# Choosing each expert's eight tokens by a threshold, and collecting the experts' outputs through DRAM, in a convolution-attention-expert kernel

## The chip, the cores and the metric

The kernel runs on one core of a Trainium2 chip. The metric is the device time of one execution in microseconds (us). Three runs of the kernel before the change took 2435.75, 2436.49 and 2438.75 us; their median, 2436.49 us, is the time to which the changed kernel is compared. The core's engines are TensorE (PE, matrix products and transposes), VectorE (DVE), ScalarE (ACT), GpSimd (POOL) and SyncE (SP, which here only issues DMAs). ACT issues DMAs too.

## What is computed

The input is x of shape (4, 128, 64, 64): 4 images of 128 channels and 4096 positions. Layer 0 is a group norm and an attention over the 4096 positions of an image. Layer 1 works on the positions as tokens of 128 numbers: a running (cumulative) attention with 8 heads, and then an expert layer in which every expert chooses its tokens:

```python
logits = jnp.einsum('bsd,ed->bse', x, gate_w) + gate_b
probs = jax.nn.softmax(logits, axis=1)
vals, idx = jax.lax.top_k(probs.transpose(0, 2, 1), K)
...
pooled = jnp.einsum('bked,bke->bed', gathered, topv)
...
h = jax.nn.gelu(jnp.einsum('ebd,edh->ebh', h, weight1), approximate=False)
...
out = jnp.einsum('ebh,eho->ebo', h, weight2)
...
outputs = outputs.at[jnp.arange(Bn)[:, None], flat_idx].add(weighted)
```

There are 64 experts (E), each takes the K = 8 tokens of an image with its highest gate logits, the softmax runs over the 4096 tokens, and x stands here for the layer-normed tokens. An expert sums its eight tokens by their probabilities into one row (pooled), passes that row through two matrices (128 to 512, GELU, 512 to 128), and adds the result, times each token's probability, to its eight tokens.

## The kernel before

Everything is in float32. Layer 0 fills the first 1460 us or so; the change does not touch it. It leaves all tokens in SBUF in the tile `t`, and for every query the sum of its softmax row in `rows`. Layer 0 leaves out the row maximum of the softmax; `test_rows` (L645) tests that all these sums lie in a safe interval and writes the verdict to `inside`. At the very end every engine loads `inside` into a register (L1304), and if it is 0 everything is computed again by a slower general path (L1305 to L1308), which calls `layer1("g_", False)`. With the inputs used here `inside` is 1. The argument `ready` of `layer1` is True in the first, fast call.

`layer1` first runs a loop over 32 blocks of 512 tokens (`loop`, L1025; n counts blocks, NB = 32, 8 blocks an image). The order of PE's instructions in it is that of the program text (`tc.manual_schedule`); the order of all other instructions, here and later, comes from a list scheduler. `gate_logits` (L929) leaves the gate logits of images 2p and 2p+1 in `lgs[p]`, a tile of 128 partitions (64 experts of two images) by 4096 tokens, and the eight largest of every 512 in `cand[p]`.

The choice has these steps, for p = 0 inside the loop (n = 18 to 26) and for p = 1 after it:

- `select` (L942): the eight largest (`top`) of the 64 candidates, minus the largest (`ng`), and six more small DVE instructions which replace in `cand[p]` every candidate that is not among the eight by a number that no logit has.
- `pick_mark` (L964), for each block k: `match_replace` on DVE copies the logits into `left` and overwrites in it one occurrence of each value of `cand[p][:, k, :]`. So ties are resolved as top_k does.
- `pick_exp` (L973): ACT takes exp(logit - maximum) in place and adds up the softmax denominator.
- `pick_keep` (L980): DVE keeps the exponentials that are marked and sets the others to 0.
- `pick_turn` and `pick_sum`: PE transposes the kept weights, DVE multiplies them by the tokens' inverse deviations (`ct`), PE adds up the weighted tokens (`pp`).

Then the pools of the loop are closed, and the space takes 19 weight buffers of 512 KB, with `wks` and `wvs` 21 (NW). `load_expert` (L1110) loads an expert's two matrices on SP's queue into buffer e modulo 21; the first 21 loads are issued as space comes free, load e + 21 when expert e has been used.

The experts are taken in 16 groups g of four (QG = 4, EG = 16). `first(g)` (L1209) multiplies the pooled rows by the four first matrices and copies the result from PSUM (`hr`, ACT). `turn(g)` (L1222) transposes it (`htr`, PE), adds the bias (`hs`, DVE) and takes the GELU (ACT). `second(g)` (L1237) multiplies by the second matrices (`po`), copies to SBUF (`og`, DVE, two buffers), issues the four loads that the group's buffers are free for, and sends the group's 16 rows (4 experts, 4 images, 512 bytes each) to `eos[p]`, where partition z*64 + e holds expert e's output for image 2p + z: four DMAs of four rows, two on SP's queue and two on ACT's (L1254). The loop (L1261) also multiplies one block of `lgs` by the softmax denominator's inverse `rden` on ACT (L1272), and turns one or two blocks of `t` to channel-major form (`backs`, L1151: four PE transposes into `otr` and one copy, by ACT or DVE). `HB` = 16 of the 32 turned blocks come before the group loop: seven while the last logits are made, nine in the loop over k (L1177).

Every engine executes its own instructions in order, and so do the DMA queues' issuing engines: an issue on ACT or SP that waits holds up what stands behind it. The built program gives every DMA that SP and ACT issue one of eight completion semaphores in turn; a DMA is only issued when the one that used its semaphore before has landed.

At the end (L1275 to L1301) DVE adds the second bias to `eos`, PE multiplies the outputs by the probabilities block by block (`sct`), DVE adds this to `t`, and SP stores the result, 24 DMAs of 256 or 512 KB.

Of the kernel before, what the change touches and what calls it, by code (L numbers as in the profile page):

```python
# [8 lines left out]
F32 = mybir.dt.float32  # L9
AF = mybir.ActivationFunctionType  # L10
# [3 lines left out]
P = 128  # L14
# [4 lines left out]
def conv_attn_hybrid_kernel(  # L19
# [623 lines left out]
    inside = resid.tile([P, 1], mybir.dt.int32, tag="inside", name="inside")  # L643

    def test_rows(sb, ps):  # L645

        ends = sb.tile([P, 4], F32, tag="ends", name="ends", bufs=1)
        nc.vector.tensor_reduce(ends[:, 0:1], rows, AX.X, ALU.min)
        nc.vector.tensor_reduce(ends[:, 1:2], rows, AX.X, ALU.max)
        nc.vector.tensor_scalar(  # L650
            out=ends[:, 2:3], in0=ends[:, 0:1], scalar1=1e-20, scalar2=None, op0=ALU.is_ge
        )
        nc.vector.tensor_scalar(
            out=ends[:, 3:4], in0=ends[:, 1:2], scalar1=1e25, scalar2=ends[:, 2:3],
            op0=ALU.is_le, op1=ALU.mult,
        )
        good = ps.tile([P, BLK], F32, tag="kv", name="good")
        nc.tensor.matmul(good[:, 0:1], all_ones, ends[:, 3:4], start=True, stop=True)
        nc.vector.tensor_scalar(  # L659
            out=inside, in0=good[:, 0:1], scalar1=float(P), scalar2=None, op0=ALU.is_ge  # L660
        )
# [11 lines left out]
    def layer1(pre, ready):  # L673

        with ExitStack() as kept, ExitStack() as l1:
# [223 lines left out]
            den = lgp.tile([P, B // 2, NBLK], F32, tag="den", name=f"{pre}den")  # L899
            rden = lgp.tile([P, B // 2], F32, tag="rden", name=f"{pre}rden")  # L900

            total = lgp.tile([P, C], F32, tag="total", name=f"{pre}total")
            gmv, grs, xgs, xts, picks, cts, lefts = {}, {}, {}, {}, {}, {}, {}
# [38 lines left out]
            def select(p):  # L942

                flat = cand[p].rearrange("p k e -> p (k e)")
                top = gp.tile([P, 8], F32, tag="top", name=f"{pre}top_{p}")
                nc.vector.max(out=top, in_=flat)
                ng = gp.tile([P, 1], F32, tag="ng", name=f"{pre}ng_{p}")
                nc.vector.tensor_scalar_mul(ng, top[:, 0:1], -1.0)
                sel = gp.tile([P, NBLK * 8], F32, tag="sel", name=f"{pre}sel_{p}")
                nc.vector.match_replace(  # L950
                    out=sel, in_to_replace=top, in_values=flat, imm_value=-LOWEST
                )
                nc.vector.tensor_scalar(
                    out=sel, in0=sel, scalar1=1e38, scalar2=None, op0=ALU.is_ge
                )
                nc.vector.tensor_mul(flat, flat, sel)
                nc.vector.tensor_scalar(
                    out=sel, in0=sel, scalar1=1.0, scalar2=3e38, op0=ALU.subtract, op1=ALU.mult
                )
                i = nc.vector.tensor_add(flat, flat, sel)  # L960
                picks[p] = ng
                return i.ins

            def pick_mark(p, k, left):  # L964

                lefts[p, k] = left
                i = nc.vector.match_replace(
                    out=left, in_to_replace=cand[p][:, k, :], in_values=lgs[p][:, bass.ts(k, BLK)],
                    imm_value=LOWEST,
                )  # L970
                return i.ins

            def pick_exp(p, k):  # L973
                lg = lgs[p][:, bass.ts(k, BLK)]
                i = nc.scalar.activation(
                    lg, lg, AF.Exp, bias=picks[p], accum_out=den[:, p, k : k + 1]
# [3 lines left out]
            def pick_keep(p, k):  # L980
                lg = lgs[p][:, bass.ts(k, BLK)]
                nc.vector.scalar_tensor_tensor(
                    out=lg, in0=lefts.pop((p, k)), scalar=-3.3e38, in1=lg,
                    op0=ALU.is_le, op1=ALU.mult,
                )
# [39 lines left out]
            def loop():  # L1025
# [3 lines left out]
                for n in range(NB):  # L1029
# [18 lines left out]
                    with ExitStack() as order:  # L1048
# [3 lines left out]
                        if 0 <= k0 < NBLK:  # L1052
                            left = gp.tile([P, BLK], F32, tag="left", name=f"{pre}left_0_{k0}")
                            order.enter_context(tc.issue_after(pick_mark(0, k0, left)))
# [48 lines left out]
            fs = pool("l2fs", 2)  # L1103
            ps_a = pool("l2a", 4, space=PSUM)
# [19 lines left out]
            eos = [fo.tile([P, C], F32, tag=f"eo{p}", name=f"{pre}eo_{p}") for p in range(B // 2)]  # L1124
# [45 lines left out]
            backs(2, nc.scalar)  # L1170
# [6 lines left out]
            for k in range(NBLK + 1):  # L1177
# [9 lines left out]
                if turns and turns[0] < HB:  # L1187
                    backs(1, nc.scalar)
# [48 lines left out]
            def second(g, hs):  # L1237
# [12 lines left out]
                by = og.rearrange("(u w) o -> w u o", u=QG)  # L1250
                for p in range(B // 2):
                    for z in range(2):
                        at = z * E + g * QG
                        (nc.scalar if p else nc.sync).dma_start(  # L1254
                            out=eos[p][at : at + QG, :], in_=by[2 * p + z]
                        )
# [4 lines left out]
            for g in range(EG):  # L1261
# [9 lines left out]
                with tc.issue_after(gelu):  # L1271
                    nc.scalar.activation(probs, probs, AF.Copy, scale=rden[:, p : p + 1])  # L1272
                second(g, hs)
            backs(len(turns), nc.vector)
            for eo in eos:  # L1275
                nc.vector.tensor_add(eo, eo, fb2s)

            for p in range(B // 2):

                for k0, OB in ((0, 1), (1, 1), (2, 2), (4, 2), (6, 1), (7, 1)):  # L1280
                    for k in range(k0, k0 + OB):
# [4 lines left out]
                        for z in range(2):  # L1286
                            half = slice(z * E, (z + 1) * E)
                            nc.tensor.matmul(
                                pss[z], eos[p][half, :], lgs[p][half, bass.ts(k, BLK)],
# [6 lines left out]
                    for z in range(2):  # L1296
                        n = (2 * p + z) * NBLK + k0
                        nc.sync.dma_start(
# [65 lines left out]
```

## Time and profile before

| What | Value |
|---|---|
| Median of three runs | 2436.49 us |
| The profiled execution: time / span of its instructions | 2434.62 / 2432.9 us |
| PE busy | 2360.8 us, 97% of the span |
| DVE, ACT, POOL busy | 1504.9, 1213.7, 304.1 us |
| `match_replace` of 512 logits (L967) | 0.676 us, plus 0.086 us to load the eight values |
| exp of 512 logits (L975) | 0.722 us, plus 0.188 us to read the sum |
| scaling of 512 probabilities on ACT (L1272) | 0.710 us |
| DMAs to `eos` | 64 of 2 KB |
| weight loads | 64 of 512 KB |

Busy time is the time in which an engine executes; the span is from the first instruction to the last. PE's matmuls are pipelined and their ends are modelled, so that a busy PE can still have been waiting in part. Times of single instructions are given as us from the start of the span. A row of the timeline gives start, duration, engine, line, operation, output and inputs, shapes and count, and in brackets the idle time of the engine before it and what ended it. A row of the waits gives who waited for whom, the total, how many times, and the longest.

### The profile page before, as it was taken

To read this page: it belongs to the slowest core of one execution; us is meant where nothing else is said; L and a number is where in the kernel's file an instruction comes from. 1 tells how busy PE (TensorE), PEld (TensorE's weight loads), DVE (VectorE), ACT (ScalarE), POOL (GpSimd) and SP (SyncE) were. 2 spreads that over 40 slices of the span, in tenths; PEclk is the share of its full clock that TensorE was granted. 3 is DMA by queue.
4 is the path that set the end of the run, shared out by engine and by line. 5 is a ranking of instruction groups with operands and counts; after the bars stand their busy time and mean duration, and the time that the engine had idled before them with its cause. 6 is when DMAs were issued, how large, how long until landed. Compare 5 with 4: busy or idle time off the path is not lost. (4 is left out here: it accounts for less than half of the span.)

```text
span 2432.9 us, 45864 instructions
## 1 busy us (share of the span) xinstructions
PE 2360.8 (97%) x19482; PEld 1569.3 (65%) x19482; DVE 1504.9 (62%) x2619; ACT 1213.7 (50%) x1631; POOL 304.1 (13%) x338
## 2 busy tenths in 40 slices
PE   6999999999999999999999998999999999999886
PEld 3567767677778677677777774555555555555543
DVE  5666666666656666655555555666666677776623
ACT  4454444444443544444434335666666666656531
POOL 0000000000000000000000002433333333333100
PEclk9999999999999999999999999999999999999899
DMA  2200120000100000200000001121211211112576
GB/s 75 79 22 11 26 61 1 11 18 22 49 23 1 22 14 18 54 13 1 1 1 1 1 1 36 37 54 37 49 43 38 53 37 50 42 37 54 201 261 255
DMA packets 61704, 110.09 MB, mean 45 GB/s; under 512 B 10288, under 2 KB 35632, under 8 KB 61488
## 3 DMA queue, kind: packets, MB, share of 16 engines
q1 hardware_dynamic: 59520, 105.48, 15.0%
q8 instruction: 154, 2.52, 0.4%
q10 hardware_dynamic: 1968, 1.58, 0.2%
q14 instruction: 62, 0.51, 0.1%
HBM read 85.40 MB, written 8.91 MB: 39 GB/s over the span
## 5 line engine op out<-in xcount | busy, mean ns | idle before, releaser
L513 PE MATMUL av<-pr,am 64*128 64x512 f32 x4096 | 1051.2, 592 | 0.7 <-ACT pr L492 0.7
L495 DVE TENSOR_TENSOR acc<-acc,pr 128x1024 f32<-128x1024 f32 x480 | 586.9, 1223 | 443.5 <-ACT pr L492 443.2
L492 ACT ACTIVATE pr<-sc 128x1024 f32<-128x1024 f32 x512 | 523.5, 1023 | 671.0 <-PE sc L488 602.2
L513 PEld LDWEIGHTS av<-pr,am 64*128 64x128 f32 x4096 | 636.9, 187 | 253.0 <-issue 31.1
L488 PE MATMUL sc<-e,e 64*128 64x512 f32 x2048 | 608.0, 592 | 0.0
L488 PEld LDWEIGHTS sc<-e,e 64*128 64x128 f32 x2048 | 315.3, 187 | 103.4 <-issue 15.9
L725 PE MATMUL pk<-xt,wks 128*128 128x512 f32 x512 | 241.5, 611 | 6.5 <-DVE inside L659 4.2
L843 PE MATMUL pv<-wvs,xt 128*128 128x512 f32 x512 | 227.3, 597 | 2.1 <-ACT v L847 2.1
L847 ACT ACTIVATE v<-pv 128x512 f32<-128x512 f32 x256 | 152.7, 597 | 70.3 <-PE pv L843 70.2
L727 ACT ACTIVATE ks<-pk 128x512 f32<-128x512 f32 x256 | 148.5, 597 | 60.1 <-PE pk L725 59.8
L843 PEld LDWEIGHTS pv<-wvs,xt 128*128 128x128 f32 x512 | 96.6, 191 | 122.1 <-issue 112.6
L831 DVE TENSOR_TENSOR em<-em,rb 128x1024 f32<-128x1024 f32 x64 | 79.0, 1235 | 146.1 <-DMA rb<-rd 146.1
L725 PEld LDWEIGHTS pk<-xt,wks 128*128 128x128 f32 x512 | 91.3, 191 | 113.1 <-issue 80.9
L822 POOL TENSOR_TENSOR em<-et,mask 128x1024 f32<-128x1024 f32 x64 | 122.4, 1934 | 85.9 <-ACT et L809 85.9
L96 POOL TENSOR_SCALAR xg<-t,gmv,grs 128x128 f32<-128x128 f32 x120 | 95.1, 805 | 288.6 <-DVE grs L92 229.7
L879 PEld LDWEIGHTS po<-v,em 64*64 64x64 f32 x4096 | 111.6, 133 | 27.3 <-DVE before L869 26.7
L879 PE MATMUL po<-v,em 64*64 64x128 f32 x4096 | 119.6, 271 | 0.3 <-issue 0.3
L733 POOL MEMSET ew<- 128x1024 f32 x1 | 1.0, 952 | 942.1 <-PE pa L455 942.1
L781 DVE RECIPROCAL rr<-rr 128x512 f32<-128x512 f32 x32 | 107.3, 3353 | 1.1
L766 ACT ACT_TABLE_LOAD x24 | 30.8, 1283 | 119.0 <-DVE ss L765 119.0
L767 POOL COPY state<-mm 128x1 f32<-128x1 f32 x32 | 20.6, 644 | 502.3 <-DVE mm L761 502.3
L869 DVE TENSOR_TENSOR before<-before,pt 128x128 f32<-128x128 f32 x256 | 72.6, 284 | 9.6 <-PE pt L859 3.8
(185 smaller groups left out, 2101.9 us busy)
## 6 DMA issues: line engine op xcount, KB each, us to landing
rb<-rd SPq DMA_DIRECT2D x128, 256.0 KB
fw<-in_fw_dram SPq DMA_DIRECT2D x58, 512.0 KB
t<-in_xtok_dram SPq DMA_DIRECT2D x32, 256.0 KB
e<-ee SPq DMA_DIRECT2D x63, 128.0 KB
x<-in_x_dram SPq DMA_DIRECT2D x14, 512.0 KB
out_dram<-t SPq DMA_DIRECT2D x16, 256.0 KB
out_dram<-t SPq DMA_DIRECT2D x8, 512.0 KB
e<-ee SPq DMA_DIRECT2D x63, 64.0 KB
```

The lines of the kernel that those rows point to most:

```text
L96: i = engine.tensor_scalar(out=dst, in0=t[:, chunk, :], scalar1=mean, scalar2=rs, op0=ALU.subtract, op1=ALU.mult)
L488: nc.tensor.matmul(sc[:, u, :], e2[halves[u], p, :], e1[halves[u], :], start=True, stop=True)
L492: nc.scalar.activation(pr, sc, AF.Exp)
L495: added.append(nc.vector.tensor_add(acc, acc, pr).ins)
L513: nc.tensor.matmul(av, am[h, j, :], pr[h, u, :], start=(j == 0), stop=(j == NCH - 1))
L725: nc.tensor.matmul(pk, wks[:, h, :], xt, start=True, stop=True)
L727: nc.scalar.activation(ks, pk, AF.Silu)
L781: inverse = nc.vector.reciprocal(rr, rr).ins
L822: nc.gpsimd.tensor_tensor(em, eq.unsqueeze(2).to_broadcast([P, 2 * NH, H2]), mask.unsqueeze(1).to_broadcast([P, 2 * NH, H2]), ALU.mult,)
L843: nc.tensor.matmul(pv.rearrange("p h d -> p (h d)"), xt[:, bass.ts(2 * q + s, P)], wvs[:, bass.ts(m, BLK)], start=True, stop=True,)
L847: last = nc.scalar.activation(v[:, bass.ts(m, HPB), :], pv, AF.Silu).ins
L879: nc.tensor.matmul(po[s * H2 : (s + 1) * H2, u, q, :], aas[q][half, s, h, :], vs[2 * q + s][half, h, :], start=(q == 0 and h == 0), stop=F ...
```

## The change

Five things are changed, all in `layer1` and for the first call unless said otherwise.

1. **Choice.** `select` stops after `top` and `ng`; the eighth largest logit is kept as `eighth[p]`. `pick_mark` does nothing but name the tile `left`; `pick_exp` writes the exponentials into `left` and leaves the logits; `pick_keep` keeps an exponential where its logit is at least `eighth[p]`. With `ready` False all is as before.
2. **Count.** A logit equal to the eighth would be chosen too, so the chosen are counted: in the group loop ACT takes the sign of a block of kept exponentials into a PSUM tile and adds it up (`count`). At the end DVE and one matmul test that no expert has more than eight, and `inside` becomes the product of this test and of the old one (now `within`). So the load of `inside` on SP, which stood early in the program, now stands ahead of the stores.
3. **Scaling.** The multiplication by `rden` goes from ACT to DVE.
4. **Outputs.** A group's `og` is written whole to a DRAM tile `ogd` (64 KB, one DMA on ACT's queue), for all groups but the last. When group 14 is written, four DMAs on SP's queue read 60 rows each from there into `eos`; the last group's 16 rows go directly, two DMAs on SP and two on ACT. `eos` is one tile, and the bias is added by one DVE instruction.
5. **Turned blocks and stores.** Two of the seven `backs` ahead of the choice go into the loop over k, whose copies must follow the exp of that k; and every second store of the result is issued by ACT in place of SP.

```diff
@@ -641,6 +641,7 @@
     inside = resid.tile([P, 1], mybir.dt.int32, tag="inside", name="inside")
+    within = resid.tile([P, 1], F32, tag="within", name="within")
@@ -657,7 +658,7 @@
         nc.vector.tensor_scalar(
-            out=inside, in0=good[:, 0:1], scalar1=float(P), scalar2=None, op0=ALU.is_ge
+            out=within, in0=good[:, 0:1], scalar1=float(P), scalar2=None, op0=ALU.is_ge
         )
@@ -897,10 +903,12 @@
+            count = lgp.tile([P, B // 2, NBLK], F32, tag="count", name=f"{pre}count")
             rden = lgp.tile([P, B // 2], F32, tag="rden", name=f"{pre}rden")
             total = lgp.tile([P, C], F32, tag="total", name=f"{pre}total")
-            gmv, grs, xgs, xts, picks, cts, lefts = {}, {}, {}, {}, {}, {}, {}
+            gmv, grs, xgs, xts, picks, eighth, cts, lefts = {}, {}, {}, {}, {}, {}, {}, {}
@@ -942,10 +950,13 @@
                 flat = cand[p].rearrange("p k e -> p (k e)")
-                top = gp.tile([P, 8], F32, tag="top", name=f"{pre}top_{p}")
+                top = gp.tile([P, 8], F32, tag=f"top{p}", name=f"{pre}top_{p}")
                 nc.vector.max(out=top, in_=flat)
-                ng = gp.tile([P, 1], F32, tag="ng", name=f"{pre}ng_{p}")
-                nc.vector.tensor_scalar_mul(ng, top[:, 0:1], -1.0)
+                ng = gp.tile([P, 1], F32, tag=f"ng{p}", name=f"{pre}ng_{p}")
+                i = nc.vector.tensor_scalar_mul(ng, top[:, 0:1], -1.0)
+                picks[p], eighth[p] = ng, top[:, 7:8]
+                if ready:
+                    return i.ins
                 sel = gp.tile([P, NBLK * 8], F32, tag="sel", name=f"{pre}sel_{p}")
@@ -958,12 +969,13 @@
                 i = nc.vector.tensor_add(flat, flat, sel)
-                picks[p] = ng
                 return i.ins
...
                 lefts[p, k] = left
+                if ready:
+                    return None
                 i = nc.vector.match_replace(
@@ -973,16 +985,22 @@
                 i = nc.scalar.activation(
-                    lg, lg, AF.Exp, bias=picks[p], accum_out=den[:, p, k : k + 1]
+                    lefts[p, k] if ready else lg, lg, AF.Exp, bias=picks[p],
+                    accum_out=den[:, p, k : k + 1],
                 )
...
                 lg = lgs[p][:, bass.ts(k, BLK)]
-                nc.vector.scalar_tensor_tensor(
-                    out=lg, in0=lefts.pop((p, k)), scalar=-3.3e38, in1=lg,
-                    op0=ALU.is_le, op1=ALU.mult,
-                )
+                left = lefts.pop((p, k))
+                if ready:
+                    nc.vector.scalar_tensor_tensor(
+                        out=lg, in0=lg, scalar=eighth[p], in1=left, op0=ALU.is_ge, op1=ALU.mult
+                    )
+                else:
+                    nc.vector.scalar_tensor_tensor(
+                        out=lg, in0=left, scalar=-3.3e38, in1=lg, op0=ALU.is_le, op1=ALU.mult
+                    )
@@ -1051,7 +1069,9 @@
                             left = gp.tile([P, BLK], F32, tag="left", name=f"{pre}left_0_{k0}")
-                            order.enter_context(tc.issue_after(pick_mark(0, k0, left)))
+                            marked = pick_mark(0, k0, left)
+                            if marked is not None:
+                                order.enter_context(tc.issue_after(marked))
                         if 1 <= k0 <= NBLK:
@@ -1101,6 +1121,9 @@
             fs = pool("l2fs", 2)
+            dram2 = l1.enter_context(
+                tc.tile_pool(name=pre + "l2dram", bufs=1, space=bass.MemoryType.DRAM)
+            )
             ps_a = pool("l2a", 4, space=PSUM)
@@ -1121,7 +1144,8 @@
-            eos = [fo.tile([P, C], F32, tag=f"eo{p}", name=f"{pre}eo_{p}") for p in range(B // 2)]
+            eos = fo.tile([P, B // 2, C], F32, tag="eo", name=f"{pre}eo")
+            ogd = dram2.tile([(EG - 1) * P, C], F32, tag="og", name=f"{pre}ogd")
             fb2s = fo.tile([P, C], F32, tag="fb2s", name=f"{pre}fb2s")
@@ -1167,7 +1191,6 @@
             select(1)
-            backs(2, nc.scalar)
             pp = ps_p.tile([P, C], F32, tag="pp", name=f"{pre}pp_1")
@@ -1184,8 +1207,10 @@
                     pick_sum(1, k - 1, pp, k == 1, k == NBLK)
-                if turns and turns[0] < HB:
-                    backs(1, nc.scalar)
+                for _ in range(2 if k < 3 else 1):
+                    if turns[0] < HB:
+                        with tc.issue_after(exp):
+                            backs(1, nc.scalar)
             divisors(1)
@@ -1247,13 +1272,19 @@
                     load_expert(g * QG + u + NW)
-                by = og.rearrange("(u w) o -> w u o", u=QG)
-                for p in range(B // 2):
-                    for z in range(2):
-                        at = z * E + g * QG
-                        (nc.scalar if p else nc.sync).dma_start(
-                            out=eos[p][at : at + QG, :], in_=by[2 * p + z]
-                        )
+                if g + 1 < EG:
+                    nc.scalar.dma_start(out=ogd[bass.ts(g, P), :], in_=og)
+                    by, of, queues = ogd, slice(0, (EG - 1) * QG), (nc.sync, nc.sync)
+                else:
+                    by, of, queues = og, slice(g * QG, E), (nc.sync, nc.scalar)
+                if g + 2 >= EG:
+                    by = by[: (of.stop - of.start) * QW].rearrange("(e w) o -> w e o", w=QW)
+                    for p in range(B // 2):
+                        for z in range(2):
+                            queues[p].dma_start(
+                                out=eos[z * E + of.start : z * E + of.stop, p, :], in_=by[2 * p + z]
+                            )
@@ -1268,12 +1299,31 @@
                 probs = lgs[p][:, bass.ts(k, BLK)]
-                with tc.issue_after(gelu):
-                    nc.scalar.activation(probs, probs, AF.Copy, scale=rden[:, p : p + 1])
+                if ready:
+                    ones_of = ps_a.tile([P, BLK], F32, tag="kv", name=f"{pre}chosen_{g}")
+                    with tc.issue_after(gelu):
+                        nc.scalar.activation(
+                            ones_of, probs, AF.Sign, accum_out=count[:, p, k : k + 1]
+                        )
+                nc.vector.tensor_scalar_mul(probs, probs, rden[:, p : p + 1])
                 second(g, hs)
             backs(len(turns), nc.vector)
-            for eo in eos:
-                nc.vector.tensor_add(eo, eo, fb2s)
+            if ready:
+                chosen = fs.tile([P, 4], F32, tag="chosen", name=f"{pre}chosen", bufs=1)
+                nc.vector.tensor_reduce(chosen[:, 0:2], count, AX.X, ALU.add)
+                nc.vector.tensor_reduce(chosen[:, 2:3], chosen[:, 0:2], AX.X, ALU.max)
+                nc.vector.tensor_scalar(
+                    out=chosen[:, 3:4], in0=chosen[:, 2:3], scalar1=8.5, scalar2=None, op0=ALU.is_le
+                )
+                good = ps_a.tile([P, BLK], F32, tag="kv", name=f"{pre}good")
+                nc.tensor.matmul(good[:, 0:1], all_ones, chosen[:, 3:4], start=True, stop=True)
+                nc.vector.tensor_scalar(
+                    out=inside, in0=good[:, 0:1], scalar1=float(P), scalar2=within,
+                    op0=ALU.is_ge, op1=ALU.mult,
+                )
+            nc.vector.tensor_add(
+                eos, eos, fb2s.unsqueeze(1).to_broadcast([P, B // 2, C])
+            )
@@ -1286,7 +1336,7 @@
                             nc.tensor.matmul(
-                                pss[z], eos[p][half, :], lgs[p][half, bass.ts(k, BLK)],
+                                pss[z], eos[half, p, :], lgs[p][half, bass.ts(k, BLK)],
                                 start=True, stop=True,
@@ -1295,7 +1345,7 @@
                         n = (2 * p + z) * NBLK + k0
-                        nc.sync.dma_start(
+                        (nc.scalar if z else nc.sync).dma_start(
                             out=out[2 * p + z, :, bass.ds(k0 * BLK, OB * BLK)],
```

## The prediction

> **What bounds the kernel now.** I read the page's slices first (PE is full until the last three), then the waits, the stretches of the end, and the timeline there. Three stages matter.
>
> ```profile
> PE   6999999999999999999999998999999999999886
> DMA  2200120000100000200000001121211211112576
> ...
> 2290.00:2310.00 20.00, 15.81 (x119) 13.61 (x117) 14.17 (x36) 13.61 (x28) 0.00 (x0) 0.78 1.01 403
> 2313.00:2326.00 13.00, 11.20 (x126) 6.59 (x124) 4.12 (x10) 3.73 (x8) 0.00 (x0) 1.00 0.00 0
> 2326.00:2392.00 66.00, 57.33 (x608) 24.99 (x606) 12.84 (x35) 20.75 (x44) 0.00 (x0) 1.00 0.94 344
> 2406.00:2430.00 24.00, 16.76 (x56) 8.26 (x52) 17.47 (x29) 0.00 (x0) 0.00 (x0) 0.86 0.91 348
> ```
>
> Columns: the stretch, its length, busy us of PE, weight load, DVE, ACT and POOL with counts, granted clock, DMA share, GB/s. The reader sees: 21 weight loads at 403 GB/s; 13 us without any, since no buffer is free; the other 43 in 66 us at 344 GB/s; the stores at 348 GB/s.
>
> ```profile
> SPq L1118 <- DMA fw<-in_fw_dram: 33.9, 36, 2.0
> SPq L1118 <- PE po L1241: 22.4, 1, 22.4
> ...
> DVE og L1247 <- DMA eo<-og: 12.6, 6, 3.2
> ```
>
> SP, issuing loads, waits 33.9 us for earlier loads (their completion semaphores) and once 22.4 us for group 0. From then on DVE waits 12.6 us for the small DMAs out of `og`.
>
> ```profile
> 2294.41 1.56 ACT L1143 COPY t<-otr 128x512 f32<-128x512 f32 x3
> 2295.99 1.28 ACT L975 ACT_TABLE_LOAD   x1
> 2297.55 0.72 ACT L975 ACTIVATE lg<-lg,ng 128x512 f32<-128x512 f32 x1 [0.28 <-DVE left L967]
> 2299.14 1.12 PE L990 MATMUL ctr<-ident,lg 128*128 128x128 f32 x4 [4.17 <-DVE lg L982]
> ...
> 2322.85 0.22 DVE L1230 TENSOR_TENSOR hs<-htr,fb1s 128x64 f32<-128x64 f32 x1 [2.57 <-PE htr L1226]
> 2326.82 0.23 DVE L1230 TENSOR_TENSOR hs<-htr,fb1s 128x64 f32<-128x64 f32 x1 [0.17 <-PE htr L1226]
> 2331.28 0.23 DVE L1230 TENSOR_TENSOR hs<-htr,fb1s 128x64 f32<-128x64 f32 x1 [0.24 <-PE htr L1226]
> 2396.93 0.21 DVE L1230 TENSOR_TENSOR hs<-htr,fb1s 128x64 f32<-128x64 f32 x1
> 2398.43 0.26 ACT L1235 ACTIVATE hs<-hs 128x64 f32<-128x64 f32 x1 [3.47 <-DMA eo<-og]
> 2399.96 0.29 DVE L1247 COPY og<-po 128x128 f32<-128x128 f32 x1 [1.47 <-PE po L1241]
> 2402.55 0.59 DVE L1276 TENSOR_TENSOR eo<-eo,fb2s 128x128 f32<-128x128 f32 x2 [2.30 <-DMA eo<-og]
> ```
>
> `hs` marks a group: the first two follow each other after 3.97 and 4.46 us (one and two turned blocks between), but the sixteenth comes 74.08 us after the first, 4.94 a group. The last GELU waits while ACT is held by its issues to `eos`.
>
> **Term 1, the choice for p = 0: 0 us.** Per block a mark (0.676 + 0.086 us of DVE) goes, per p six small instructions (1.26 us, 2295.47 to 2296.73). In the loop PE is busy 26.00 of 26.00 us in the stretches with a choice (DVE 19.45), and an iteration there takes 26.37 us against 24.95 after it, by the distance of the reciprocals of L781. The 1.42 more is about PE's own turn and sum (0.44 + 0.95 at their pitch), so DVE's marks lie beside it. Were that cover gone, 8 x 0.76 + 1.26 = 7.3 us would come back; I keep 0.
>
> **Term 2, the choice for p = 1: -1.7 us.** The first exp stood behind three copies (1.56 us) and the mark. In the changed program it follows the last logits (ACT done 2294.38) and the table load: 2295.7, with `ng` there at 2295.56. With its 0.72 + 0.1 us, a keep of 0.69 and 0.1 us of hand-over PE starts `ctr` at 2297.4, not 2299.14. From there PE's work is the same (seven turned blocks stay ahead, nine in the loop); its only waits until 2320 are 1.1 + 0.3 us, so DVE's freed 0.76 a block gives little. Lower end 0 (copies now behind exps hold PE's buffers up). The other end hangs on the clock: after the pause of 4.17 us it stands at half.
>
> ```profile
> 2294.00:2298.00 4.00, 0.98 (x9) 0.74 (x7) 3.34 (x13) 3.68 (x6) 0.00 (x0) 1.00 1.03 414
> 2302.00:2306.00 4.00, 4.00 (x29) 3.50 (x27) 3.27 (x8) 2.36 (x6) 0.00 (x0) 0.57 1.02 405
> ```
>
> Half speed from 2298.6 to 2305.5 costs about 3.4 us. Near 2264 pauses of 1.59 and 0.83 us were followed by half speed too, so I assume that a pause of 2.4 us keeps the penalty; without it the term is -5.1. *The Trainium skill, "TensorE: Matmul & The Clock Gate", Part 1, says that half speed follows an idle window of some 3.4 us; by that rule the shorter pause can escape, and the whole sum would be 3.4 us lower; the row at 2264 speaks against it.*
>
> **Term 3, the sixteen groups: -6.7 us.** (a) Weights. Each group had four small DMAs beside four loads, all on eight semaphores, so that four loads were in flight; now there is one write, so about 6.4. At the 403 GB/s of the first stretch a load takes 1.30 us, 43 take 55.9; ten writes of 64 KB add 10 x 0.16 to 0.22, some 2. That is 58 us for 66. (b) So the groups' own pace decides. In the built program `second(g)` now stands right behind `turn(g)`, no longer one or two groups later. Groups 0 to 5 keep the pace seen: 3 x 3.97 + 3 x 4.46 = 25.3 us. From group 6 on `hr` stands on ACT behind the write of `og`, which waits for DVE's copy, that for PE: bias 0.3, GELU 0.3, `po` 1.06 with one matmul of the next group 0.4, copy 0.4, issue 0.5, `hr` 0.7, `htr` 0.66, or 4.35 us; nine such are 39.2, and seven turned blocks in front of `po` add 7 x 0.52 = 3.6. In all 68.1 us from first to last `hs` instead of 74.1: -6.0. The weights fit: loads from 2324.5 to 2382.6, last `hs` at 2389.3. (c) From the last `hs` to the end of `og` 3.3 us become 2.6 (bias 0.23, GELU 0.3, sign 0.71 + 0.19, scaling by DVE 0.43 to 0.53 as at L415 and L407, two reductions 0.3, copy 0.29): -0.7. The sign costs ACT 0.19 more a group than the scaling did and loads no table in the built program; beside this chain it is hidden, and what waits behind it is only DVE's scaling and `og`. Bounds: +8 (see the second rival) to -9 (4.1 us in each late group).
>
> **Term 4, the way into `eos`: -0.1 us.** Group 14's `og` is ready 4.5 us before the last. A write to DRAM shows 1.8 us from its last issue to the waiting read's issue (L789 at 2008.4, L796 at 2010.17), and an issue to `eos` takes 0.54: so SP's four reads go out from 2.2 us before the last `og` to its end, and its two own DMAs right behind: the last is issued 0.65 us after `og`, and 1.73 us later (2400.82 to 2402.55 before) the bias starts, 2.4 us for 2.3; the one addition saves about 0.2. The nearest row for the reads, L796 at 2010.17 to `em` at 2015.06, gives up to 4.9 us, and that end makes the term +2.1. I take the small DMA's price, since 30 KB is nearer to 2 KB than the 256 KB per issue of L796. The count's test (three small DVE steps of 0.15 to 0.2, one matmul) lies in that wait; with a longer chain it would cost its own 1 us. SP's load of `inside` (1.03 us where ACT did it) ends before the first store, which comes 4 us after `og`.
>
> **Term 5, stores on two queues: 0 us.** 8.4 MB leave at 391 to 405 GB/s once they flow, and DVE's 32 additions set the rest; the last four issues on SP took 0.82 to 1.40 us where 0.33 is usual, so up to 1.5 us could go; +0.5 if the queues disturb each other. *The Trainium skill, "DMA: Bandwidth & Descriptors", Rules for kernel authors, says that spreading DMAs over engines brings no bandwidth, only issue time; by it the term is 0, by the row up to -1.5.*
>
> **Sum.** 0 - 1.7 - 6.7 - 0.1 + 0 = -8.5. The profiled execution took 2434.62 (span 2432.9), so 2426.1; it lies 1.87 below the median of the three, so the forecast is 2436.49 - 8.5 = **2428.0 us**, with a range of its own of 2422 to 2432.
>
> **Rivals.** *The loads gain nothing*: 66 us again, because the small DMAs never were what slowed them. For it: the DMA share is 0.94 already. Against: 403 GB/s at a share of 1.01 just before. Then the last load lands at 2390.5, `hs` follows after 2.5, `og` 2.6 later at 2395.6 instead of 2400.25: -4.75, **2431.7**.
> *ACT's order makes the groups the bound, slower than before*: the write of `og` ahead of `hr` also waits for its semaphore, that is for a load, and for DVE. For it: ACT was held 3.47 us that way before the last GELU. Against: the load it waits for is needed for the next `first` anyway. `hs` of group 6 would be at 2346.5; nine groups pass the old end (2400.25 - 2.6) from 5.7 us each on. At 6.6 us they give `og` at 2408.5, +8.2, **2444.7**.
> *The change doesn't hold*: the sign of a zero counts, the test fails, and the general path runs. That repeats at least both layers: some **4870 us**. Nothing in the profile speaks to it.
>
> **How the numbers follow.** Forecast 0.63, first rival 0.20, second 0.15, third 0.02. The three runs lie within 0.12%, so 0.2% (4.9 us) is about what can be told from no change: faster means below 2431.6. The forecast's range lies nearly all there (0.60), the first rival about half (0.09): 0.69. Within: 0.03 + 0.11 + 0.02 = 0.16; slower: 0.13 + 0.02 = 0.15. The range, 2421.5 to 2437, takes in the first rival, the bound of term 4, and half speed escaped; left out are most of the second rival, the third, and both best ends at once.
>
> **What would show it.** `ctr` starting near 2297.4 and, with or without half speed after it, term 2; 43 loads in about 58 us; distances of `hs` near 4.0 to 4.5 up to group 6 and 4.4 to 5.3 from there; `eo` 2.4 us after the last `og`; the same 26.37 us per iteration in the loop. Wrong it is if late groups take over 5.7 us, or if the wait of `eo` grows by more than 2.

## The result, and the profile after

The changed kernel takes 2437.23 us (median of 4 runs, 2436.81 to 2438.51) against 2436.12 us for the kernel before on the same chip (4 runs, 2432.69 to 2438.75): a ratio of 1.0006 with a 95% interval of 0.9989 to 1.0024. That is no change. The forecast was 8.5 us less. The profiled execution of the changed kernel took 2438.51 us, its span is 2436.8 us, against 2432.9 before.

The span can be cut at marks that both kernels have, each the start of an instruction: the first reciprocal of layer 1's loop, the last one, ACT's copy of the last logits (L945; L937 before), the first `ctr`, the `hs` of groups 0, 6 and 15, the last copy to `og`, the (first) addition to `eos`, the first store. Two more columns are of experiments told below: the changed kernel with POOL issuing the writes of `og`, and a second profile of the unchanged changed kernel.

| Stretch, us | before | changed | changed, writes on POOL | changed, again |
|---|---|---|---|---|
| start to first reciprocal | 1479.66 | 1480.60 | 1480.68 | 1479.18 |
| loop, first to last reciprocal | 784.32 | 785.54 | 785.97 | 783.69 |
| to the last logits | 29.72 | 31.39 | 28.20 | 29.45 |
| to `ctr` | 5.44 | 3.65 | 3.65 | 3.65 |
| to `hs` of group 0 | 23.71 | 24.57 | 24.18 | 24.06 |
| groups 0 to 6 | 25.96 | 20.92 | 20.94 | 20.93 |
| groups 6 to 15 | 48.13 | 53.28 | 46.70 | 52.73 |
| to the last `og` | 3.02 | 1.89 | 1.89 | 1.90 |
| to `eos` with its bias | 2.59 | 3.86 | 4.00 | 3.92 |
| to the first store | 2.28 | 3.34 | 3.34 | 3.34 |
| to the end | 28.06 | 27.74 | 27.50 | 27.63 |
| span | 2432.9 | 2436.8 | 2427.1 | 2430.5 |
| 43 loads, first issue to last landing | 66.99 | 68.34 | 61.79 | 67.80 |

In the sixteen groups 5.04 us are won early and 5.15 lost late. Three views of the changed kernel show where. First its slices of the span, then stretches of the end (columns as in the prediction):

```profile
PE   6999999999999999999999998999999999999886
DMA  2200120000100000200000001121211212112577
```

```profile
2291.00:2312.00 21.00, 18.17 (x118) 15.09 (x118) 9.56 (x19) 16.08 (x32) 0.00 (x0) 0.69 1.02 408
2316.00:2329.00 13.00, 10.77 (x121) 6.07 (x119) 4.53 (x11) 3.11 (x7) 0.00 (x0) 1.00 0.00 0
2329.00:2397.00 68.00, 60.01 (x673) 27.94 (x672) 20.63 (x53) 22.25 (x60) 0.00 (x0) 1.00 0.94 347
2355.00:2363.00 8.00, 7.04 (x87) 3.16 (x85) 2.55 (x7) 2.08 (x6) 0.00 (x0) 1.00 1.03 416
2364.00:2370.00 6.00, 5.14 (x55) 2.46 (x54) 1.70 (x4) 2.04 (x5) 0.00 (x0) 1.00 0.83 262
2409.00:2433.00 24.00, 17.80 (x60) 8.38 (x56) 18.59 (x31) 0.00 (x0) 0.00 (x0) 0.93 0.92 349
```

Slices and stretches are nearly those of before. The 43 loads still take 68 us at 347 GB/s. Within them the rate is uneven: 416 GB/s over 8 us, then 262 over 6. The transfers themselves are as fast as they were in the first 21 loads; something leaves them without work. The second view is of SP's waits from 2326 to 2398:

```profile
SPq L1141 <- DMA ogd<-og: 33.1, 10, 6.2
SPq L1141 <- PE po L1266: 26.4, 5, 24.6
...
SPq L1141 <- DMA fw<-in_fw_dram: 4.8, 5, 1.3
```

Before, in the same stretch, the wait that ended last for a load was nearly always that for an earlier load, and twice that for a small DMA:

```profile
SPq L1118 <- DMA fw<-in_fw_dram: 23.8, 27, 2.0
...
SPq L1118 <- DMA eo<-og: 4.0, 2, 2.0
```

(The 33.9 us in 36 waits that stand ahead of the prediction's terms are of all loads from 2283 us on; the 43 have 23.8 of them.) Now ten loads wait 33.1 us for a write of `og`, up to 6.2 us each. The third view is the timeline around one of them, ACT first, then SP:

```profile
2357.43 0.33 ACTq L1277 DMA_DIRECT2D ogd<-og  x1
2357.89 0.59 ACT L1244 COPY hr<-ph 128x512 f32<-128x512 f32 x1 [1.29 <-PE ph L1239]
2359.54 0.26 ACT L1260 ACTIVATE hs<-hs 128x64 f32<-128x64 f32 x1 [1.06 <-DVE hs L1255]
...
2357.39 8.03 SPq L1141 DMA_DIRECT2D fw<-in_fw_dram  x4
```

ACT issues the write of group 7 at 2357.43 and goes on at once with `hr`: the write does not hold ACT. SP, in the same place, needs 8.03 us for four issues. The trace's DMA records take them apart (us; issue and last byte landed):

```
load 42          issued 2357.39  landed 2366.15
write of og_7    issued 2357.43  landed 2363.65
load 43          issued 2363.72  landed 2367.57   <- 0.07 after the write
load 44          issued 2364.16  landed 2370.49
```

(Load e is that of expert e.) Load 43 has the completion semaphore that the write of `og_7` used before it. Its buffer has been free since group 5, whose `og` was written at 2346.68. But when the write is issued, loads 37 to 42, issued from 2352.81 on, are still under way; its first packet moves at 2360.91, and its 64 KB have landed 6.22 us after issue (the 15 writes: 1.5 to 7.8 us, median 5.7). SP executes in order, so load 44 and all behind it wait too, and from 2364 to 2370 the queues are short of work. The same is seen at load 28 (buffer free at 2332.8, write of `og_1` landed 2339.74, issue 2339.80), load 34 (2339.86, `og_4` at 2350.72, issue 2350.79) and load 51 (2357, `og_9` at 2375.00, issue 2375.07). In the built order loads 28, 34, 43, 51, 54 and 58 follow, on their semaphore, the writes of groups 1, 4, 7, 9, 10 and 11; their buffers are freed by groups 1, 3, 5, 7, 8 and 9. ACT's writes, on the other hand, wait for no semaphore: each one's had been free for 4.7 us or more when it was issued.

### The profile page after: what moved, and what is told of

The parts are those of the page before. It is cut to its first block, busy times and chain, and to the rows that moved or that the text cites. A ratio compares the mean times of both kernels' runs of the same rounds, so it can differ in the third digit from the quotient of the medians.

```text
span 2436.8 us, 45779 instructions
## 1 busy us (share of the span) xinstructions
PE 2366.7 (97%) x19484; PEld 1573.5 (65%) x19484; DVE 1502.5 (62%) x2594; ACT 1214.6 (50%) x1647; POOL 304.3 (12%) x338
## 4 chain that ended last, share of the span: by engine, by line
```

## Experiments

Each was timed beside runs of the kernel before on the same chip, and a ratio is to these; it is worked out from all runs and need not be the quotient of the medians (which are: 2435.35 us of 29 runs for the first two, "The way through DRAM alone, ACT's writes" and "The rest of the change alone"; 2438.18 of 26 for SP's writes, "The way through DRAM alone, POOL's writes" and the first edit of the last group's DMAs; 2436.89 of 20 for the other three). SP's waits are those at L1141 from 2326 us or a little earlier to the end of the loads.

### POOL issues the writes

```diff
-                    nc.scalar.dma_start(out=ogd[bass.ts(g, P), :], in_=og)
+                    nc.gpsimd.dma_start(out=ogd[bass.ts(g, P), :], in_=og)
```

> The changed kernel, but the fifteen writes of og to DRAM are issued by POOL instead of ACT; they then have semaphores of their own, and the loads follow only each other on the eight. Theory (coupled loads): in the changed kernel a write of 64 KB lies behind the loads already issued and takes 4.8 to 7.8 us, and the load that takes over its semaphore, with all loads behind it on SP, waits for it, so that the transfers run dry; then here the 43 loads after the first 21 take 56 to 61 us instead of 68.3, the late groups 5.0 to 5.4 us instead of 5.92, and the time is 2429 to 2433 us. Rival (ACT's order): the late groups are slow since hr stands behind the write on ACT; ACT is relieved here too, so this run alone does not tell it from the theory: 2428 to 2432. Second rival (buffers): the loads wait for the buffers of earlier groups anyway; then 66 to 69 us again and 2435 to 2438.

2428.96 us (6 runs), ratio 0.997 (0.9958 to 0.9982): 0.3% less than before, with an interval that leaves out 1. The 43 loads take 61.79 us, a little more than the 56 to 61 that the theory gave, and the time lies just under its 2429. Their stretch, and then SP's waits in it:

```profile
2326.00:2388.00 62.00, 56.10 (x674) 27.50 (x674) 20.97 (x53) 22.19 (x60) 7.81 (x15) 1.00 0.97 380
```

```profile
SPq L1141 <- DMA fw<-in_fw_dram: 28.6, 31, 1.4
SPq L1141 <- PE po L1266: 23.3, 6, 20.2
```

No load waits for a write any more; SP's longest wait for an earlier load is 1.4 us, about the 1.28 to 1.30 us in which one load passes. 380 GB/s instead of 347, and 5.19 us for a late group, which is four loads at that pace. So the loads now set it. One line of code is worth what the forecast had promised for the groups: 20.94 + 46.70 + 1.89 = 69.5 us, against 77.1 before, is -7.6. That this is near the forecast's -6.7 is luck in part: groups 0 to 6 are 4.4 us faster than it had them, the nine late ones 3.9 slower.

### `hr` ahead of the write on ACT

```diff
+            copies = {}
...
-                nc.scalar.copy(hr, ph)
+                copies[g] = nc.scalar.copy(hr, ph)
...
-                    nc.scalar.dma_start(out=ogd[bass.ts(g, P), :], in_=og)
+                    with tc.issue_after(copies[g + 1].ins):
+                        nc.scalar.dma_start(out=ogd[bass.ts(g, P), :], in_=og)
```

> The changed kernel, with the write of og(g) behind hr(g+1) on ACT in every group; the DMAs, their number and their semaphores stay. Theory (coupled loads): the writes still hold the loads up, 43 loads in 66 to 70 us, late groups 5.7 to 6.1 us, time within 0.1% of the changed kernel (2435 to 2439). Rival (ACT's order): late groups fall to 4.4 to 5.2 us and the time to 2427 to 2431.

2434.42 us (12 runs), ratio 0.9993 (0.9984 to 1.0002); loads 64.85 us, late groups 48.86 us (5.43 each). Both expectations missed: the late groups lie between them, the time just under the theory's 2435, and the loads just under its 66. SP's waits say why the edit did not cure them:

```profile
SPq L1141 <- DMA ogd<-og: 30.0, 10, 4.5
SPq L1141 <- PE po L1268: 25.3, 4, 23.0
```

Still ten waits for a write. Why they cost less here, 3 us in sum, was not taken apart.

### ACT's order kept, its DMA gone

```diff
-                    nc.scalar.dma_start(out=ogd[bass.ts(g, P), :], in_=og)
+                    nc.gpsimd.dma_start(out=ogd[bass.ts(g, P), :], in_=og)
+                    nc.scalar.copy(fs.tile([P, C], F32, tag="aside", name=f"{pre}aside_{g}", bufs=1), og)
```

POOL writes, and ACT copies `og` to a tile that nobody reads, at the place where it had issued the write. So ACT waits for DVE's `og` ahead of the next `hr` as in the changed kernel, but has no semaphore and no transfer to share.

> The changed kernel with POOL's writes, and on ACT, at the places where the changed kernel issues its writes, a copy of og into a tile that nobody reads: ACT so waits for og(g) ahead of hr(g+1) as in the changed kernel, while the loads wait for no write. Theory (the loads' waits for writes are the cost, ACT's order costs only through them): 43 loads in 61 to 63 us, the nine late groups 46 to 48 us, time within 1.5 us of POOL's writes alone (2428 to 2432). Rival (ACT's order has a price of its own): late groups 49 to 52 us, time 2432 to 2435.

2430.91 us (8 runs), ratio 0.9973 (0.9962 to 0.9983); loads 61.82 us, late groups 46.35 us. SP's waits:

```profile
SPq L1141 <- DMA fw<-in_fw_dram: 28.5, 30, 2.1
SPq L1141 <- PE po L1266: 26.1, 5, 23.0
```

ACT's wait for `og` ahead of `hr` costs nothing by itself. With the writes' semaphores free in time (above), this clears the suspect of the second rival.

### SP issues the writes

```diff
-                    nc.scalar.dma_start(out=ogd[bass.ts(g, P), :], in_=og)
+                    nc.sync.dma_start(out=ogd[bass.ts(g, P), :], in_=og)
```

> The changed kernel, with the writes of og to DRAM issued by SP, behind the loads that their group sets free; ACT has no DMA in the group loop, while writes and loads still share eight semaphores in turn. Theory (coupled loads): the loads still wait for writes that lie behind earlier loads, 43 loads in 64 to 69 us, late groups 5.5 to 6.1 us, time 2433 to 2438. Rival (ACT's order alone costs the late groups their time): late groups at most 5.3 us as with POOL's writes, 2428 to 2431.

2434.38 us (11 runs), ratio 0.9984 (0.9975 to 0.9993). The time is in the range expected, but the loads are not slow: 62.47 us, late groups 45.20. SP's waits:

```profile
SPq L1141 <- PE po L1266: 30.9, 8, 23.0
SPq L1277 <- DVE og L1272: 19.5, 9, 4.0
SPq L1141 <- DMA fw<-in_fw_dram: 5.9, 8, 0.9
```

Writes and loads still share the eight semaphores. But here a load follows, in the built order, the write of a group that is two earlier than the one that frees its buffer (load 4k + 31 follows the write of group k), and no load waits for a write's landing. So sharing alone is not the harm; it is sharing in an order in which the write comes later than the buffer. SP now waits for DVE's `og` instead, and the price falls elsewhere. Groups 0 to 6 take 24.27 us (20.92 in the changed kernel), and at the end the writes of groups 12 to 14 and the reads from `ogd` stand late on SP, so that the last `og` comes 3.23 us after the last `hs` (1.89) and the bias 5.02 us after it (3.86).

### The way through DRAM alone, ACT's writes

```diff
+            ogd = dram2.tile([(EG - 1) * P, C], F32, tag="og", name=f"{pre}ogd")
...
-                by = og.rearrange("(u w) o -> w u o", u=QG)
...
+                if g + 1 < EG:
+                    nc.scalar.dma_start(out=ogd[bass.ts(g, P), :], in_=og)
+                    by, of, queues = ogd, slice(0, (EG - 1) * QG), (nc.sync, nc.sync)
...
```

The kernel before, with part 4 of the change only.

> The kernel before, with only the way into eos changed (fifteen writes to DRAM, four reads, four own DMAs, one addition); the choice and the stores as before. Theory (coupled loads): the 43 loads take 66 to 70 us as in the changed kernel, and the time is that of the kernel before within 0.15% (2433 to 2439). Prediction's term 3: weights in 58 us, the last hs some 6 us earlier, 2428 to 2431.

2436.25 us (12 runs), ratio 1.0001 (0.999 to 1.0011); loads 69.45 us, late groups 53.77 us. Both the early gain (groups 0 to 6 in 21.61 us) and the late loss come with part 4 and need nothing of the other choice.

### The rest of the change alone

```diff
-            eos = fo.tile([P, B // 2, C], F32, tag="eo", name=f"{pre}eo")
-            ogd = dram2.tile([(EG - 1) * P, C], F32, tag="og", name=f"{pre}ogd")
+            eos = [fo.tile([P, C], F32, tag=f"eo{p}", name=f"{pre}eo_{p}") for p in range(B // 2)]
...
-                        (nc.scalar if z else nc.sync).dma_start(
+                        nc.sync.dma_start(
```

The changed kernel with the old sixty-four small DMAs and all stores on SP.

> The changed kernel, with the way into eos and the stores of the kernel before: only the choice by the eighth largest logit, its count, and the scaling on DVE. Theory: the choice saves 1 to 2 us ahead of ctr and a further 0.5 in the loop, part of it lost again before the first group; groups as in the kernel before, 43 loads in 65 to 68 us; time 2432 to 2436. Rival (the sign on ACT and the scaling on DVE lengthen the groups): groups over 5.1 us on average and 2437 to 2441.

2437.40 us (11 runs), ratio 1.0001 (0.9992 to 1.001). `ctr` starts 1.79 us earlier after the last logits, as in the changed kernel, and nothing is left of it in the time; the section "Why the prediction was wrong, point by point" says where it goes. The time and the loads (68.24 us) missed the theory's 2432 to 2436 and 65 to 68. The time lies in the rival's range, but the rival's sign is missing: the groups took 5.02 us on average (4.94 before), not over 5.1.

### The way through DRAM alone, POOL's writes

The same edit of the kernel before, with the writes on POOL:

```diff
-                    nc.scalar.dma_start(out=ogd[bass.ts(g, P), :], in_=og)
+                    nc.gpsimd.dma_start(out=ogd[bass.ts(g, P), :], in_=og)
```

> The kernel before, its choice and its stores, with the way into eos through DRAM and the writes on POOL. Theory: the choice by the eighth logit brings nearly nothing, since what it saves ahead of ctr goes again before the first group; so this kernel is within 1.5 us of the changed kernel with POOL's writes: 2427.5 to 2431, 43 loads in 60 to 63 us. Rival (the choice is worth the predicted 1.7 us and the stores 0.5): 2431 to 2433.

2430.34 us (9 runs), ratio 0.9968 (0.9957 to 0.998); loads 62.53 us, late groups 47.40 us. The same ratio as with the whole change and POOL's writes: the new choice adds nothing that can be measured.

### The last group's DMAs

The changed kernel takes 3.9 us from the start of the last `og` to that of the addition to `eos`, 4.0 with POOL's writes, and 2.6 us before. Of the last four small DMAs two are on SP and two on ACT:

```profile
2401.84 0.29 DVE L1272 COPY og<-po 128x128 f32<-128x128 f32 x1
...
2402.16 1.16 SPq L1285 DMA_DIRECT2D eo<-og  x2
2402.21 1.96 ACTq L1285 DMA_DIRECT2D eo<-og  x2
2405.70 0.42 DVE L1324 TENSOR_TENSOR eo<-eo,fb2s 128x256 f32<-128x256 f32 x1 [2.75 <-DMA eo<-og]
```

ACT's two issues take 1.96 us (1.38, a gap of 0.04, and 0.54), SP's 1.16. With POOL's writes, one of ACT's two goes to SP:

```diff
-                            queues[p].dma_start(
+                            (queues[p] if z else nc.sync).dma_start(
```

> The changed kernel with POOL's writes, and of the last group's four small DMAs into eos three on SP and one on ACT instead of two each. Theory: ACT's first small DMA in this stretch takes 1.38 us to issue, and its second so lands last; with three on SP the last lands some 3.1 us after og's copy begins, eo starts 3.1 to 3.4 us after it instead of 4.0, and the time is 0.5 to 1 us lower, which may lie within the scatter: 2427 to 2429.5. Rival (the wait is that of the transfers, not of the issue): 4.0 us again.

2431.74 us (11 runs), ratio 0.9972 (0.9963 to 0.9981); 4.04 us from `og` to `eos`, a miss, as is the time. SP's third DMA landed 2.34 us after its issue. At 2396.27, while it was under way, an instruction packet of 8 KB (queue 14) ran for 0.49 us, 0.97 us after POOL's branch instruction. In the changed kernel such a packet starts at 2404.52 (branch at 2403.55) and meets ACT's second DMA, which lands 2.04 us after issue. In the two kernels with the old choice and the way through DRAM, where POOL does not branch there, it lands after 1.58 and 1.59 us, and `eos` comes 3.38 and 3.44 us after `og`.

So the branch was moved: POOL branches on `inside`, and if DVE writes `inside` only after the addition to `eos`, branch and packet come later.

```diff
-                nc.vector.tensor_scalar(
-                    out=inside, in0=good[:, 0:1], scalar1=float(P), scalar2=within,
-                    op0=ALU.is_ge, op1=ALU.mult,
-                )
-            nc.vector.tensor_add(
+            summed = nc.vector.tensor_add(
...
+            if ready:
+                with tc.issue_after(summed.ins):
+                    nc.vector.tensor_scalar(
+                        out=inside, in0=good[:, 0:1], scalar1=float(P), scalar2=within,
+                        op0=ALU.is_ge, op1=ALU.mult,
+                    )
```

> The changed kernel with POOL's writes, and the last step of the test (the write of inside) behind the addition to eos. Theory: in the changed kernel POOL and SP read inside as soon as it is there and branch, and the 8 KB instruction packet that this fetches lies ahead of packets of the last small DMA into eos; then here eo starts 3.3 to 3.5 us after the last og instead of 4.0, and the time falls by 0.3 to 0.6 us, within the scatter (2428 to 2431). Rival (the last DMA is late for another reason): 4.0 us again.

2430.84 us (7 runs), ratio 0.9972 (0.9961 to 0.9983). The timeline of DVE in this kernel:

```profile
2395.34 0.29 DVE L1272 COPY og<-po 128x128 f32<-128x128 f32 x1
...
2398.80 0.42 DVE L1320 TENSOR_TENSOR eo<-eo,fb2s 128x256 f32<-128x256 f32 x1 [3.11 <-DMA eo<-og]
2399.14 0.21 DVE L1325 TENSOR_SCALAR inside<-good,within 128x1 int32<-128x1 f32 x1
```

3.46 us from `og` to `eos` (2395.34 to 2398.80), as expected, and the last small DMA takes 1.60 us. The half microsecond is seen in the trace; in the time it is below what can be told.

### The changed kernel again

The changed kernel, without an edit.

> The changed kernel as it is, once more, with more runs beside the kernel before and a second profile. Expected: within 0.1% of the kernel before (ratio 0.999 to 1.001); 43 loads in 66 to 69 us, SP waiting some 30 us for the writes of og; the number of 3.41 us stretches at half clock may differ from the first profile.

2436.76 us (11 runs), ratio 1.0 (0.9991 to 1.0009). Its profile has a span of 2430.5 us where the first had 2436.8, with the loads again at 67.80 us and SP waiting 37.0 us for writes. The mechanism repeats; the 6.3 us between the two spans lie elsewhere, 5.2 of them before the last logits (table above). One of the places is the start of layer 1's loop, in the first profile and in this one:

```profile
1479.00:1486.00 7.00, 4.98 (x12) 2.32 (x12) 4.73 (x3) 4.51 (x8) 1.73 (x2) 0.76 0.01 2
```

```profile
1478.00:1485.00 7.00, 5.34 (x16) 2.66 (x17) 6.13 (x4) 5.36 (x10) 3.18 (x3) 1.00 0.01 2
```

The granted clock, third from the right, is 0.76 in the one and 1.00 in the other: 3.41 us at half speed, and the first iteration took 23.59 us instead of 21.90.

No experiment is clearly faster than POOL's writes alone (0.997): with the tail's edits, with ACT's copy or with the old choice the ratios lie at 0.9968 to 0.9973, within each other's intervals. Not tried: keeping all `og` in SBUF, and the two edits of the tail together.

## Why the prediction was wrong, point by point

**Term 1 (0 us) held.** Most of the loop's iterations with a choice take 26.29 us instead of 26.37, some 0.5 us over the loop. The loop is 1.22 us longer in the first profile all the same, because of one more stretch at half clock at 1481.50; the second profile has none there and is 0.63 us shorter than before.

**Term 2 (-1.7 us): its first step right, its second not.** `ctr` starts 3.65 us after the copy of the last logits begins instead of 5.44 (2293.70 to 2299.14), -1.79:

```profile
2297.53 0.68 ACT L945 ACTIVATE lg<-pl,gbs 64x512 f32<-64x512 f32 x1 [1.05 <-PE pl L941]
...
2301.18 1.12 PE L1008 MATMUL ctr<-ident,lg 128*128 128x128 f32 x4 [2.81 <-DVE lg L997]
```

The step that failed is "From there PE's work is the same": PE has 215 matmuls between `ctr` and the first `hs` where it had 211 (one turned block more), and waits 0.7 to 1.8 us for `ct` where it waited 0.3. In the first profile that leaves -0.93 from the last logits to the first `hs`. Four profiles have a single stretch of 3.41 us at half clock between the last logits and the first `hs`, and among them nothing is left: 27.76 and 27.77 us with the old choice, 27.71 and 27.83 with the new one. Half speed remained in the first profile, as assumed: 6.8 us from 2300.7 on, as before from 2298.6. In the second it was 3.41 us, but so it was in the two with the old choice and the old pause, so the shorter pause is not shown to be the reason.

**Term 3 (-6.7 us) is where the forecast fell.** The step that failed is 3(a): "now there is one write, so about 6.4 in flight", hence 58 us for 66. The count of small DMAs was right, and that they were worth removing too: with POOL's writes the loads take 61.8 us and the term measures -7.6. What the working left out is where the one write stands in the order of issue. It shares a semaphore with a load whose buffer is free long before, it is issued while earlier loads are under way and lands up to 7.8 us later, and SP waits in order. The loads took 68.3 us instead of 58. Even with the writes on POOL they take 61.8, and why not 58 was not taken apart. (b) Groups 0 to 5 needed 20.9 us, not the 25.3 written down, for which the old pace was kept; that gain comes with part 4 (21.61 with it alone, 25.88 without it); which of its effects brings it was not taken apart. The nine late groups took 53.3, not 42.8, set by the loads and not by ACT. (c) 1.13 us came back after the last `hs`, not 0.7. In sum the term measured 5.04 - 5.15 + 1.13, or -1.0 us.

**Term 4 (-0.1 us)** measured +1.27, inside its bound of +2.1. The step that failed is "the last is issued 0.65 us after `og`": it is issued 1.49 us after the end of `og`, since ACT's first small issue takes 1.38 us where the others take 0.53 to 0.58, and it lands 2.04 us later instead of 1.58, which the instruction packet accounts for. The reads from DRAM were done in time. No run removes both.

**Term 5 (0 us)** measured -0.32; the kernels with stores on two queues end 27.5 to 28.2 us after the first store, those on SP alone after 28.1 to 28.5, so the gain is not clear of the scatter. (The rows from 2410 us on give 385 to 405 GB/s, not 391 to 405.) The additional 1.06 us ahead of the first store is hardly the change's: the stretch takes 3.2 to 3.4 us in every later profile, also with part 4 alone and with everything but part 4 and the stores of part 5, two kernels that share no part of the change. It is 2.28 only in the one profile of before, where the half clock began 1.9 us after the addition to `eos`; in the others it began ahead of it or with it.

**The rivals.** The first, loads that gain nothing, had the loads' time right (66 us said, 68.3 measured) and its reason wrong: the small DMAs did slow them. The second put the loss into ACT's order; late groups passed its break-even of 5.7 us (5.92 each), but the early ones had saved 5 us, ACT's writes waited for no semaphore, and with ACT's order kept and its DMA taken away nothing is lost.

**The sum.** -0.5 - 0.9 - 1.0 + 1.3 - 0.3 is about -1.4 us for the change's own parts; what is left to the +3.9 between the spans is 0.94 before layer 1, 1.67 ahead of the last logits, 1.06 ahead of the first store and 1.7 in the loop; in the first, second and last of these the two profiles of the changed kernel differ as much. Over all runs of both kernels no difference remains.

## What to carry to other kernels

When DMAs of two engines share a small set of completion semaphores, count not only how many there are but who stands ahead of whom: a late, small write in the turn of an early load holds that load, and in-order issue holds all loads behind it. Look at the waits of the issuing engine's queue for the name of another engine's transfer, and move that transfer to a queue whose completions are apart (here POOL's: a ratio of 0.997, 0.9958 to 0.9982, for one line). A saving found at one end of a bounded stage, here 5 us in the early groups, is worth nothing until the stage's bound moves too.

## What the runs showed of the hardware

- A write of 64 KB from SBUF to DRAM, issued while loads of 512 KB are queued, landed after 1.5 to 7.8 us (median 5.7); the 1.54 us are those of the last one, which had no load left before it from 0.3 us after its issue on. For ten of the fifteen SP waited, and issued the next load 0.06 to 0.09 us after the write had landed. The Trainium skill, "DMA: Bandwidth & Descriptors", section "Anatomy of one DMA — SWDGE (gpsimd) path", says that DMA engines do not wait on semaphores and that the issuing sequencer does so before dispatch; the 33.1 us of SP's waits agree with that.
- Half clock (a granted clock of 0.50) comes in stretches of 3.41, 6.83 or 10.24 us, but for the last one at the end, and not always in the same places: two profiles of the changed kernel have 47.3 and 37.1 us of it within their spans of 2436.8 and 2430.5. From the last reciprocal to the last logits all kernels have one such stretch at the start; with no further one they take 28.2 to 28.5 us, with 3.41 us more of it 29.4 to 29.8 and with 6.83 more 31.4 to 31.7. The Trainium skill, "TensorE: Matmul & The Clock Gate", Part 1, speaks of a free-running window of 4096 cycles, about 3.4 us; the lengths agree.
- The first small DMA that ACT issues after the last group took 1.38 us to issue, the next 0.54; on SP they took 0.52 to 0.59 each.
- In the changed kernel a branch on POOL is followed 0.97 us later by an instruction packet of 8 KB, and ACT's second 2 KB transfer, under way then, lands 2.04 us after its issue; in the three kernels where POOL does not branch in that time it lands after 1.58 to 1.60 us.
